# Two-step graph network on one core: attention ends without waiting for the adjacency product, ten dense blocks in layer 1, two copies per block on VectorE, and a new order

## The chip, the cores and the metric

The kernel runs on one core of a Trainium2 chip, as one launch. The metric is the device time of an execution in microseconds. The engines are called by their names in the profile: PE (TensorE, matmuls and transposes, with its weight loads as PEld), DVE (VectorE), ACT (ScalarE), POOL (GpSimd, which here issues gathers by index and adds one vector per block) and SP (SyncE, which issues the plain DMAs).

## What is computed

There are 3327 nodes with 256 features and an adjacency matrix `adj` of 3327 x 3327 that is about 0.24% full, with a full diagonal of random weights. Cut to what matters:

```python
# layer 0, h = relu(layernorm(x))
Xf = Xa = h
for n in range(2):                       # step 0 and step 1
    A  = top_p_attention(Xa)             # softmax of q k^T, entries kept to 90% of each row's mass
    Xf = R @ Xf                          # R = rows of (adj + I), normalized
    Xa = A @ Xa
    Z  = Z + Xf @ U1[n].T + Xa @ U2[n].T
x = x + layernorm(h + Z) * gamma + beta
# layer 1
h = relu(layernorm(x))
x = x + relu((D^-1/2 adj D^-1/2 @ h) @ W.T + b)
```

All arrays are float32.

## The kernel before

**Blocks.** The nodes are cut into 26 blocks of 128 rows. Each step treats the 26 blocks one after another, and each block has two halves that hardly depend on each other: the attention half and the adjacency half.

**The attention half** (kinds `ATT_0` and `ATT_1`, function `attention`). PE makes a block's logits in two groups (`lg0`, `lg1`), ACT takes their exponential (`ex0`, `ex1`; tile `e`, 128 x 3327), and the threshold that keeps 90% of each row's mass is searched: ACT passes over the whole row (`ev1r`, `ev1s`, in step 1 also `ev2s`; tile `ja`), small steps between them (`mass`, `tail`, `st1`, `sec`), then a DVE pass that cuts out a window (`win`), the largest entries of 16 pieces (`wm0` to `wm3`), a sort (`sort`), the exact cut (`cut`), and a DVE pass that drops what is not kept (`drop`). Then the 26 square pieces of the row block are transposed by PE in seven groups (`tr0` to `tr6`, tile `p_t`, two PSUM buffers), each group is copied out of PSUM (`atc0` to `atc6`, tile `at`, three buffers, all on ACT), and PE sums the products with the nodes (`att0` to `att6`, tile `att_acc`). The passes of neighbouring blocks overlap: while one block is transposed, the next one's window is cut and the one after that is evaluated.

**The adjacency half.** Since a row of `adj` has few entries, a block's columns are listed: DVE finds which of the 26 square pieces of each row are not zero and builds lists of indices (kind `LISTING`; pieces `flag`, `listA`, `owners`, `rows`), POOL gathers eight tiles of adjacency rows by index (`ga0` to `ga7`), and SP stores them to HBM (`store`, `ac_hbm`). The product loads the tiles again (`lda`), POOL gathers the eight matching tiles of node rows (`gv0` to `gv7`), and PE sums eight products (`adj0` to `adj7`, tile `adj_acc`). Sixteen tiles hold gathered node rows. In step 0 this is the kind `FIRST` (it stores `y`, which step 1 gathers, by `stxf`), in step 1 the kind `SECOND`.

**The end of a block in step 1.** `SECOND` loads `y` and the nodes `h` (`load_second`), scales its product and adds a kept product (`scale`, tile `hz_r`, one buffer), adds `h` (`resid0`) and stores the sum to `hz_hbm` (`sthz`). The attention half of the same block loads that sum (`ldh`), adds its own result (`resid0` of `ATT_1`), and goes on with the layer norm, the addition of `x`, the second norm and the nodes `hn` of layer 1 (`resid1`, `resid2`, `root1`, `xbet`, `input20` to `input23`, `root2`, `node2`, `stn`).

**Layer 1.** Eight of the blocks (`DENSE`) are computed as whole rows (kind `WHOLE`): SP loads the block's 1664 KB of adjacency (`row`), and PE sums 26 products in two parts (`first`, `second`) with the `hn` that lie in SBUF. The other 18 (kind `LATE`) use the lists: eight gathers of `hn` rows on POOL (`gath`) and eight products (`prod`). Both then transpose, multiply by W, add and store (`turn`, `mt`, `out`, `add`, `st`).

**The order.** Nothing is scheduled by the hardware or by the framework: every piece of work has a key, and the pieces are emitted in the order of their keys, which fixes the order of instructions on each engine and on SP's and POOL's queues. An engine that reaches an instruction whose input is missing waits, with all that is behind it. The key of a piece of block i is

```python
        at = BASES[kind] + PERIODS[kind] * (i if n is None else n) + (SHIFTS[kind][i] if kind < len(SHIFTS) else 0.0)
        for name, piece in do.items():
            plan.add(at + places[name], piece)
```

`PLACES` holds a place for each piece of a kind, `MOVED` other places for single blocks, and `EVENTS` single pieces (`nodes`: loading the nodes of step 1; `hn`: taking tiles for layer 1's nodes). The keys are only used for sorting. Before, `SHIFTS` has lists for the first five kinds.

Lines of the profile that are used below: L927 the ACT passes, L1126 the copies `atc`, L1120 the transposes, L1135 the attention products, L702 the sparse products, L678 and L692 the gathers of adjacency and node rows, L1106 `drop`, L1056 `wm`, L976 the first of the `tail` operations, L749 a DVE copy out of PSUM in the start of the kernel.

Of the kernel before, what the change touches and what calls it, by code (L numbers as in the profile page):

```python
# [10 lines left out]
F32 = mybir.dt.float32  # L11
# [3 lines left out]
ALU = mybir.AluOpType  # L15
AX = mybir.AxisListType

P = 128
# [30 lines left out]


# [55 lines left out]
BASES = (-1.892, 870.475, -13.053, -5.69, 853.823, -80.36, 1720.169, 1724.788)  # L106
PERIODS = (30.0573, 29.8334, 30.2195, 29.6001, 29.4593, 1.6, 11.4611, 29.3857)
ATT_0, ATT_1, LISTING, FIRST, SECOND, START, LATE, WHOLE = range(8)

DENSE = (0, 4, 7, 10, 13, 16, 19, 22)  # L110
# [8 lines left out]
        ldq=-44.287, lg0=-38.973, ex0=-25.597, lg1=-20.538, ex1=-16.452, guess0=-16.41, guess1=-16.131,  # L119
        guess2=-15.977, guess3=-15.603, guess4=-14.457, guess5=-14.33, guess6=-12.806, guess7=-12.277, ev1r=-11.76,  # L120
        ev1s=-8.469, st10=-7.961, guess8=-7.057, st11=-6.906, st12=-5.943, st13=-4.39, st14=-3.503, st15=-3.334,
        st16=-1.613, st17=0.027, thr=0.214, st18=0.892, win=3.72, cut0=7.309, wm1=9.04, wm0=10.134, wm3=10.495,
        wm2=12.344, sort0=14.201, sort1=14.201, sort2=15.126, sort3=16.348, sort4=16.684, sort5=17.022, sort6=18.245,
        sort7=18.909, sort8=19.469, sort9=19.668, cut1=19.862, cut2=20.795, cut3=21.407, cut4=22.022, cut5=22.834,
        drop=23.642, tr0=26.604, atc0=29.007, tr2=31.084, att0=32.223, atc2=32.504, tr1=33.541, atc1=35.266,
        inv=37.184, tr3=38.707, att1=40.1, tr4=41.126, atc3=41.825, att2=42.068, tr5=43.428, atc4=44.771,
        atc5=46.924, att3=47.519, tr6=48.685, atc6=50.691, att4=50.866, att5=51.309, edge=51.319, att6=52.006,
        attend=54.3, xtk_t=56.039, xtk_c=58.125, k_m=61.105, cut6=61.775, k_c=62.744, q_c=63.484, xu_m=65.976,
        xu_c=67.312, stxt=75.943, stq=77.565, stxu=81.473,
    ),  # L130
    dict(
        ldq=-120.275, lg0=-63.07, lg1=-47.295, ex0=-46.566, ex1=-41.634, guess0=-41.061, guess1=-39.487,
        guess2=-38.859, guess3=-38.65, guess4=-38.64, guess5=-37.462, guess6=-37.063, ev1s=-36.233, half=-35.672,
        mass0=-35.413, ev1r=-35.055, mass1=-32.043, tail0=-31.473, tail1=-31.053, tail2=-30.763, tail3=-28.525,
        mass2=-28.221, st10=-26.599, st11=-25.175, st12=-24.135, aux2=-23.815, ev2s=-21.461, st13=-18.043,
        btw1=-17.852, st14=-15.208, aux0=-14.988, aux1=-14.22, sec10=-12.922, sec11=-12.131, sec12=-10.743,
        thr=-7.89, sec13=-7.788, nt2=-2.992, win=2.783, wm2=6.046, wm0=6.444, wm1=6.454, wm3=6.526, sort0=8.121,
        sort1=8.162, sort2=9.437, sort3=10.527, sort4=11.217, sort5=12.023, sort6=12.773, sort7=13.564, sort8=15.249,
        cut0=15.328, sort9=15.348, cut1=16.458, cut2=17.341, cut3=18.102, cut4=18.886, cut5=19.961, cut6=20.011,
        drop=23.999, tr0=28.827, atc0=29.172, tr4=29.605, tr1=32.779, att0=32.801, tr2=32.803, atc1=33.007,  # L140
        att1=33.809, atc4=34.739, tr3=34.759, atc2=36.727, att2=37.933, tr5=38.539, tr6=39.45, atc3=40.18,
        att3=40.29, ldx=44.319, atc5=45.361, atc6=45.991, ldh=48.128, att4=48.571, inv=49.727, att5=50.339,
        att6=51.666, resid0=55.38, resid1=57.694, resid2=60.354, root1=64.136, xbet=66.296, input20=67.759,
        input21=69.483, edge=70.892, input22=73.309, input23=75.045, root2=79.569, node2=90.831, stn=94.821,
    ),
    dict(
        lda1=-109.475, flag1=-107.627, lda0=-103.644, flag0=-103.479, lda2=-99.182, flag2=-95.097, lda3=-93.033,
        flag3=-91.637, listA0=-89.556, listA1=-88.513, listA2=-87.593, listA3=-85.627, listA4=-84.042,
        listA5=-82.074, listN=-79.419, listA6=-78.234, listA7=-76.609, listA8=-73.622, before=-72.858,
        beforec=-71.255, owners0=-68.498, owners1=-67.041, owners2=-61.176, shared=-58.045, lentc=-56.671,  # L150
        rows0=-54.48, rows1=-53.784, rows2=-53.518, rows3=-52.901, rows4=-51.266, rows5=-50.983, rows6=-48.224,
        rows7=-41.568, ga1=-9.65, ga3=-5.744, ga5=-1.138, ga6=-0.012, ga7=0.9, ga4=0.953, ga2=3.801, ga0=3.89,
        store=12.996,
    ),
    dict(
        gv3=36.873, gv6=37.71, gv1=38.549, gv0=39.478, gv5=41.654, gv2=42.696, lda=49.308, ldg=49.654, gv4=49.849,
        gv7=50.182, adj0=50.797, adj1=50.94, adj2=53.03, adj3=56.206, adj4=57.968, adj5=59.203, adj6=62.128,
        adj7=63.299, roots=65.636, prop=66.557, mixy=74.549, stxf=84.692,
    ),
# [38 lines left out]
    ),  # L198
)

MOVED = {
    (0, 25): dict(
        stxt=114.064, stxu=154.091,
    ),
# [1570 lines left out]
```

## Time and profile before

| | |
|---|---|
| median of 11 runs | 1632.02 us (1624.22 to 1634.39) |
| the profiled execution | 1632.13 us, span 1630.4 us |
| mean granted clock of PE | 0.969 |
| busy: PE, DVE, ACT, POOL | 1482.1, 1219.2, 1135.4, 1035.3 us |
| chain by engine | PE 40%, ACT 32%, DVE 9%, DMA 7%, issue 4%, POOL 3% |
| moved by DMA | 272.26 MB, mean 167 GB/s |

By time, the first some 110 us prepare keys and nodes, step 0 runs to about 780, step 1 to about 1410, and layer 1 to the end. A window is a stretch of the span in us; beside it stand its length, the busy time of each engine with the number of instructions in it, the granted clock of PE, the busy share of the DMA engines and the GB/s. A row of waits names who waited, for whom, and the total, the number and the longest. A row of groups gives line, engine, operation and tiles, the count, the busy time, the mean of one in ns, and the idle time ahead of it.

### The profile page before, as it was taken

To read this page: it belongs to the slowest core of one execution; us is meant where nothing else is said; L and a number is where in the kernel's file an instruction comes from. 1 tells how busy PE (TensorE), PEld (TensorE's weight loads), DVE (VectorE), ACT (ScalarE), POOL (GpSimd) and SP (SyncE) were. 2 spreads that over 40 slices of the span, in tenths; PEclk is the share of its full clock that TensorE was granted. 3 is DMA by queue.
4 is the path that set the end of the run, shared out by engine and by line. 5 is a ranking of instruction groups with operands and counts; after the bars stand their busy time and mean duration, and the time that the engine had idled before them with its cause. 6 is when DMAs were issued, how large, how long until landed. Compare 5 with 4: busy or idle time off the path is not lost.

```text
span 1630.4 us, 24877 instructions
## 1 busy us (share of the span) xinstructions
PE 1482.1 (91%) x7372; PEld 1158.3 (71%) x7372; DVE 1219.2 (75%) x3963; ACT 1135.4 (70%) x2692; POOL 1035.3 (64%) x808
## 2 busy tenths in 40 slices
PE   4967999979999998998589999999999999999996
PEld 2535787767778777786367777777777777888784
DVE  4579999779999997984389888988898889601111
ACT  2657777757787786873789999999999998200000
POOL 0058888788888888887455665466556564067774
PEclk9968999989999999999889999999999999999998
DMA  6556867666566765544433334343343344377763
GB/s 183 172 166 196 271 208 230 197 192 211 165 196 197 221 209 176 165 133 160 158 119 124 122 96 126 119 125 95 112 136 117 109 138 138 127 238 267 256 190 117
DMA packets 149167, 272.26 MB, mean 167 GB/s; under 512 B 29603, under 2 KB 94496, under 8 KB 148000
## 3 DMA queue, kind: packets, MB, share of 16 engines
q1 hardware_dynamic: 109456, 181.58, 34.1%
q0 software_dynamic: 33536, 87.08, 18.5%
q10 hardware_dynamic: 6032, 1.93, 0.5%
q8 instruction: 60, 0.98, 0.2%
q14 instruction: 83, 0.68, 0.1%
HBM read 221.08 MB, written 49.41 MB: 166 GB/s over the span
## 4 chain that ended last, share of the span: by engine, by line
PE 40%; ACT 32%; DVE 9%; DMA 7%; issue 4%; POOL 3%; DVEq 0%; SPq 0%; POOLq 0%; ACTq 0%
PE att_acc L1135 14%; ACT ja L927 13%; ACT e L883 5%; PE late_sums L1544 5%; PE adj_acc L702 4%; PE p_t L1120 4%; PE p_l L866 4%; ACT at L1126 4%; PE late_acc L702 3%; DMA ac<-in_adj_t,a_idx 3%; POOL ac L678 2%; DVE cand L1056 2%; DMA vg<-hn_hbm,v_idx 2%; DMA vg<-gb_hbm,v_idx 1%; DVE e L1106 1%
## 5 line engine op out<-in xcount | busy, mean ns | idle before, releaser
L692 POOL DMA_INDIRECT vg<-y_hbm,v_idx x208 | 321.0, 1543 | 245.4 <-PE adj_acc L702 181.1
L927 ACT ACTIVATE ja<-e,t 128x3327 uint8<-128x3327 f32 x127 | 389.6, 3068 | 0.7
L678 POOL DMA_INDIRECT ac<-in_adj_t,a_idx x208 | 282.1, 1356 | 147.5 <-DVE own L619 84.4
L1135 PE MATMUL att_acc<-h,at 128*128 128x256 f32 (+1 forms) x1352 | 324.2, 386 | 0.0
L1135 PE MATMUL att_acc<-xa,at 128*128 128x256 f32 (+1 forms) x1352 | 320.7, 381 | 0.2 <-DVE hz L1250 0.2
L692 POOL DMA_INDIRECT vg<-gb_hbm,v_idx x208 | 268.2, 1289 | 63.4 <-issue 39.6
L1135 PEld LDWEIGHTS att_acc<-h,at 128*128 128x128 f32 (+1 forms) x1352 | 252.8, 193 | 41.0 <-issue 7.6
L1135 PEld LDWEIGHTS att_acc<-xa,at 128*128 128x128 f32 (+1 forms) x1352 | 251.8, 191 | 31.6 <-DVE hz L1250 0.4
L1126 ACT COPY at<-p_t 128x512 f32<-128x512 f32 (+1 forms) x364 | 196.8, 545 | 94.6 <-PE p_t L1120 89.2
L1120 PE MATMUL p_t<-ident,e 128*128 128x128 f32 x1352 | 208.4, 280 | 36.0 <-ACT at L1126 21.3
L1056 DVE MAX8 cand<-w 128x8 f32<-128x208 f32 x832 | 238.5, 358 | 0.2
L702 PE MATMUL adj_acc<-vg,ac 128*128 128x257 f32 (+1 forms) x832 | 230.1, 389 | 8.8 <-DMA vg<-gb_hbm,v_idx 6.2
L1120 PEld LDWEIGHTS p_t<-ident,e 128*128 128x128 f32 x1352 | 162.4, 143 | 93.3 <-ACT at L1126 33.0
L866 PE MATMUL p_l<-kt,q 64*128 64x512 f32 (+1 forms) x832 | 183.9, 558 | 30.0 <-ACT e L883 27.8
L1049 DVE SCALAR_TENSOR_TENSOR w<-e,t 128x3327 f32<-128x3327 f32 x52 | 191.1, 3676 | 19.9 <-ACT t L897 19.6
L1106 DVE SCALAR_TENSOR_TENSOR e<-e,kept 128x3327 f32<-128x3327 f32 x52 | 191.9, 3691 | 0.5
L883 ACT ACTIVATE e<-p_l 128x2048 f32<-128x2048 f32 x104 | 161.6, 1554 | 18.8 <-PE p_l L866 16.8
L702 PEld LDWEIGHTS adj_acc<-vg,ac 128*128 128x128 f32 x832 | 148.4, 192 | 34.6 <-issue 8.6
L692 POOL DMA_INDIRECT vg<-hn_hbm,v_idx x144 | 136.8, 950 | 54.6 <-issue 33.9
L866 PEld LDWEIGHTS p_l<-kt,q 64*128 64x128 f32 x832 | 75.5, 193 | 113.2 <-issue 67.6
L730 ACT COPY xt_k<-p_turn 128x256 f32<-128x256 f32 x52 | 19.0, 369 | 155.8 <-PE p_turn L726 154.3
L570 DVE TENSOR_REDUCE most<-adj_sb 128x7 f32<-128x896 f32 x104 | 105.2, 1012 | 4.8 <-DMA adj_sb<-in_adj_t 4.0
(443 smaller groups left out, 1924.5 us busy)
## 6 DMA issues: line engine op xcount, KB each, us to landing
ac<-ac_hbm SPq DMA_DIRECT2D x70, 512.0 KB
adj_sb<-in_adj_t SPq DMA_DIRECT2D x78, 448.0 KB
ac_hbm<-ac SPq DMA_DIRECT2D x26, 512.0 KB
adj_row<-in_adj_t SPq DMA_DIRECT2D x8, 1664.0 KB
adj_sb<-in_adj_t SPq DMA_DIRECT2D x26, 320.0 KB
gb_hbm<-gb SPq DMA_DIRECT2D x26, 256.0 KB
gb<-gb_hbm SPq DMA_DIRECT2D x26, 256.0 KB
q<-q_hbm SPq DMA_DIRECT2D x104, 32.0 KB
```

Of the source, the lines that this page charges most:

```text
L678: nc.gpsimd.indirect_dma_start(s["list"][:, k, :], None, adj_rows, bass.IndirectOffsetOnAxis(ap=s["a_idx"][:, k : k + 1], axis=0))
L692: nc.gpsimd.indirect_dma_start(t[:, :D], None, hbm[:, :], bass.IndirectOffsetOnAxis(ap=v_idx[:, i, k : k + 1], axis=0))
L702: nc.tensor.matmul(s["acc"][:, :width], s["ac"][:, k, :], rows[:, :width], start=(k == 0), stop=(k == SLOTS - 1))
L866: nc.tensor.matmul(pl[:, at : at + cw], s["q"][rows, :], kt[rows, c0 + c : c0 + c + cw], start=True, stop=True)
L883: nc.scalar.activation(halves(s["e"])[:, :, c0 : c0 + w], logits_of(s.pop(("l", g)))[:, :, :w], AF.Exp, accum_out=s["zp"][:, g : g + 1],)
L927: nc.scalar.activation(junk, s["e"][:, :N], f, bias=s["t"], scale=-1.0, accum_out=s[name])
L1049: nc.vector.scalar_tensor_tensor(w[:, :N], ev, s["t"], ev, op0=ALU.is_le, op1=ALU.mult, accum_out=s["below"])
L1056: nc.vector.max(s["cand"][:, 8 * n : 8 * n + 8], s["w"][:, c0 : c0 + cw])
L1106: nc.vector.scalar_tensor_tensor(ev, ev, kept8[:, step * NB + i, 0:1], ev, op0=ALU.is_ge, op1=ALU.mult, accum_out=den)
L1120: nc.tensor.transpose(pt[:, c : c + P], s["e"][:, b * P : (b + 1) * P], ident)
L1126: nc.scalar.copy(at[:, :w], pt[:, :w])
L1135: nc.tensor.matmul(s["att"][:, :D], at[:kb, c : c + P], v[b][:kb, :D], start=(b == 0), stop=(b == NB - 1))
```

## The change

- In step 1 the copies `atc2` and `atc5` of each block are made by DVE (`AT_VECTOR`).
- For blocks 0 to 19 (`FLIPS = 20`) the end of the block is turned around: the attention half no longer loads the product's sum but `h`, adds its result and stores that to `hz_hbm`; a new kind `NORM`, with keys of its own, loads it, adds it to the product's sum (now in two buffers), and does the norms and the rest. For blocks 20 to 25 the end stays with the attention.
- `DENSE` has ten blocks, 12 and 24 are added; 16 blocks stay with the lists.
- Every base, period, place, shift and event is new. The shifts of `FIRST` now rise from 10 to 173 and those of `SECOND` fall from 159 to 8 (53 for the last block), where both changed little over the blocks; those of `LISTING` rise from 55 to 106, where they fell from 49 to 19. `NORM` falls from 154 to -97 over its 20 blocks. `START`, `LATE` and `WHOLE` have shifts too.

```diff
+AT_VECTOR = (2, 5)
-BASES = (-1.892, 870.475, -13.053, -5.69, 853.823, -80.36, 1720.169, 1724.788)
-PERIODS = (30.0573, 29.8334, 30.2195, 29.6001, 29.4593, 1.6, 11.4611, 29.3857)
-ATT_0, ATT_1, LISTING, FIRST, SECOND, START, LATE, WHOLE = range(8)
-DENSE = (0, 4, 7, 10, 13, 16, 19, 22)
+BASES = (-1.211, 869.963, -13.315, 19.408, 853.008, -80.36, 1725.639, 1718.681, 871.362)
+PERIODS = (30.045, 29.955, 30.2736, 28.584, 29.0064, 1.6, 11.2176, 30.9758, 29.9036)
+ATT_0, ATT_1, LISTING, FIRST, SECOND, START, LATE, WHOLE, NORM = range(9)
+FLIPS = 20
+DENSE = (0, 4, 7, 10, 13, 16, 19, 22, 12, 24)
...
-        gv3=36.873, gv6=37.71, gv1=38.549, gv0=39.478, gv5=41.654, gv2=42.696, lda=49.308, ldg=49.654, gv4=49.849,
-        gv7=50.182, adj0=50.797, adj1=50.94, adj2=53.03, adj3=56.206, adj4=57.968, adj5=59.203, adj6=62.128,
+        gv7=-7.92, gv1=0.845, gv0=10.048, gv5=14.251, gv6=26.524, gv3=43.864, gv4=44.513, gv2=46.75, lda=47.649,
+        adj0=53.814, adj1=55.177, adj2=55.686, ldg=57.795, adj3=58.657, adj4=59.088, adj5=60.784, adj6=62.621,
...
-    keys=-32.591, centre=764.748, roots=817.644, hn=827.229, nodes=878.278, last_nodes=918.935, hn_last=1606.3,
+    keys=-23.287, centre=778.673, nodes=824.15, last_nodes=913.762, hn=1041.506, roots=1047.764, hn_last=1290.252,
...
-    def attend_copy(s, g):
+    def attend_copy(s, g, step):
         pt = s.pop(("pt", g))
         s["at"][g] = at = work.tile([P, 512], F32, name="at", bufs=3)
         w = (min(4 * g + 4, NB) - 4 * g) * P
-        nc.scalar.copy(at[:, :w], pt[:, :w])
+        if step == 1 and g in AT_VECTOR:
+            nc.vector.tensor_copy(at[:, :w], pt[:, :w])
+        else:
+            nc.scalar.copy(at[:, :w], pt[:, :w])
...
-        for name, hbm, tag in (("y", y_hbm, "xf1"), ("h", h_hbm, "hl")):
+        for name, hbm, tag in (("y", y_hbm, "xf1"), ("h", h_hbm, "hl"))[: 1 if i < FLIPS else 2]:
...
-        r["hz"] = work.tile([P, D], F32, name="hz_r", bufs=1)
+        r["hz"] = work.tile([P, D], F32, name="hz_r", bufs=2)
...
+    def load_attended(i, r):
+        r["h"] = work.tile([P, D], F32, tag="hl", name="h", bufs=2)
+        nc.sync.dma_start(r["h"], hz_hbm[i * P : (i + 1) * P])
+
+    def attended_node(i, t):
+        hz = t["hz"]
+        nc.vector.scalar_tensor_tensor(hz, t.pop("att")[:, :D], t["inv"], hz, op0=ALU.mult, op1=ALU.add)
+        yield
+        nc.sync.dma_start(hz_hbm[i * P : (i + 1) * P], t.pop("hz"))
...
-        nc.sync.dma_start(t["hz"], hz_hbm[i * P : (i + 1) * P])
+        nc.sync.dma_start(t["hz"], (h_hbm if i < FLIPS else hz_hbm)[i * P : (i + 1) * P])
...
-        do["resid0"] = lambda: add_node(r)
-        do["sthz"] = lambda: store_residual(i, r)
+        if i >= FLIPS:
+            do["resid0"] = lambda: add_node(r)
+            do["sthz"] = lambda: store_residual(i, r)
+        return do
+
+    def normalized(i, s, hn):
+        do = {}
+        do["ldz"] = lambda: load_attended(i, s)
+        do["plus"] = lambda: add_node(s)
+        do["ldx"] = lambda: s.update(x=load_x(i))
+        do["xbet"] = lambda: add_bet(s)
+        in_steps(do, "resid", 2, lambda: moments_in_steps(s, s["hz"]))
+        do["root1"] = do["root2"] = lambda: root_moments(s["n"])
+        in_steps(do, "input2", 4, lambda: input_2(i, s))
+        do["node2"] = lambda: node_2(i, s, hn[i])
+        do["stn"] = lambda: store_2(i, s, hn[i])
         return do
...
+        do["ldh"] = lambda: load_residual(i, s)
+        if i < FLIPS:
+            in_steps(do, "resid", 2, lambda: attended_node(i, s))
+            return do
...
             plan_block(plan, SECOND, i, products_1(i, state[SECOND, i]))
             plan_block(plan, ATT_1, i, block_1(i, state[ATT_1, i], xa1, kt2, hn))
+            if i < FLIPS:
+                plan_block(plan, NORM, i, normalized(i, state[SECOND, i], hn))
```

## The prediction

> **What bounds the kernel now.** I read the page's busy shares and its forty slices first, to see where no engine is full; then the table of windows by stage; then the chain and the waits of each stage; then the costliest groups, for prices. The profiled execution took 1632.13 us around a span of 1630.4, and the median of the runs shown is 1632.02, so a change of the span is read straight as a change of the median. About 0.2% (3.3 us) is what a measurement of this kernel can tell from no change.
>
> ```profile
> PE 1482.1 (91%) x7372; PEld 1158.3 (71%) x7372; DVE 1219.2 (75%) x3963; ACT 1135.4 (70%) x2692; POOL 1035.3 (64%) x808
> PE   4967999979999998998589999999999999999996
> DVE  4579999779999997984389888988898889601111
> ACT  2657777757787786873789999999999998200000
> POOL 0058888788888888887455665466556564067774
> ```
>
> There are three regimes: step 0 (slices 3 to 18), where PE and DVE are both high, step 1 (slices 20 to 33), where ACT stands at 9, and layer 1 (from slice 34), where only PE and POOL work.
>
> ```profile
> core 0: us, PE busy (x) PEld busy (x) DVE busy (x) ACT busy (x) POOL busy (x), PEclk, DMA share, GB/s
> 125.50:758.50 633.00, 594.47 (x3094) 469.57 (x3094) 563.12 (x1846) 469.41 (x1169) 514.77 (x389) 0.98 0.62 195
> 221.50:605.50 384.00, 364.26 (x1907) 288.96 (x1904) 349.41 (x1150) 289.91 (x723) 311.79 (x238) 0.99 0.64 200
> 888.50:1282.50 394.00, 378.63 (x1938) 296.48 (x1937) 348.90 (x1140) 382.40 (x850) 228.77 (x153) 1.00 0.39 118
> 1371.90:1421.40 49.50, 48.02 (x249) 41.37 (x248) 36.55 (x123) 17.88 (x45) 2.18 (x3) 1.00 0.38 125
> ...
> 1431.50:1611.50 180.00, 170.99 (x798) 144.48 (x796) 29.35 (x65) 11.61 (x33) 136.27 (x144) 1.00 0.71 230
> 1611.50:1630.40 18.90, 6.67 (x19) 4.68 (x18) 2.33 (x6) 0.37 (x1) 0.49 (x1) 0.61 0.14 45
> ```
>
> The first window runs from the first to the last pass of step 0 that drops the unkept entries; the second holds 15 of its blocks (25.6 us each, DVE busy 23.3: the time is 1.10 of the fullest engine). The third holds 17 blocks of step 1: 23.18 us each, ACT busy 22.49, DVE 20.52; the time is 1.03 of the fullest engine. In 1431.5 to 1611.5 POOL issues 144 gathers in 180 us, 1.25 us each without a gap, and after the last of them 18.9 us follow in which PE has 19 matmuls: layer 1 ends by POOL.
>
> ```profile
> by line: PE att_acc L1135 24.1%; PE adj_acc L702 8.0%; DMA ac<-in_adj_t,a_idx 7.6%; issue 6.6%; PE p_t L1120 6.6%; PE p_l L866 6.5%; DVE cand L1056 4.3%; DVE e L1106 3.5%; DMA vg<-gb_hbm,v_idx 2.9%; POOL vg L692 2.7%; POOL ac L678 2.6%; ACT
> ```
>
> This is the chain in the first window. Gathers are on it (7.6 + 2.9% as transfers, 2.7 + 2.6% as issues): 15.8% of 633, some 100 us. That is why step 0 runs at 1.10 and not at 1.03.
>
> ```profile
> DVE tail_d L976 <- ACT mass L897: 34.4, 17, 3.0
> L1126 ACT COPY at<-p_t 128x512 f32<-128x512 f32 x102 | 57.7, 566 | 0.3 <-PE p_t L1120 0.3
> L749 DVE COPY xt_key<-p_turn 128x256 f32<-128x256 f32 x26 | 10.8, 415 | 0.6 <-PE p_turn L726 0.2
> ```
>
> In the step 1 window DVE waits 2.0 us per block for ACT, once per block, and ACT waits for nobody: ACT sets step 1.
>
> **Step 0: the lag of the first half (term A).** The key of FIRST's block i grows by 28.584 plus its shift, 35.1 per block over the step, where the attention's grows by 29.4; before, 29.4 against 29.8. Counted in the order that the keys give, 160 of the first half's products stand ahead of step 0's last drop, where 196 did: 36 x 2 matmuls of 0.216 us (26 took 5.61) are 15.6 us off PE, 10 DVE operations of 0.48 are 5 us off DVE, and 33 node and 18 adjacency gathers are 51 x 1.25 = 64 us off POOL. DVE stays the fullest at 558. What matters is the distance: adjacency tiles are gathered, stored and loaded again, and the product that reads them stood under one block behind its attention; now it stands two behind at block 5 and five at block 20, and the node gathers' keys spread over 55 units, where they spread over 13. The gathers' 100 us on the chain can give back nothing (633 stays as 1.124 of DVE's work: -5) or all down to step 1's ratio (558 x 1.03 = 575: -58). I take a quarter, -25: SP's stores and loads of these tiles still stand in one queue, and with PE at 94% the chain falls to PE at once. The moved halves go to the passage between the steps, where three slices of PE (733 to 856 us) show 8, 5 and 8; ACT is full there, so they cost nothing as long as they don't stand ahead of its logits on PE.
>
> **Step 1: copies, second half, block ends (term B).** Two of seven copies leave ACT: 2 x 0.566 = 1.13, so 22.49 becomes 21.4 (21.5 with what is left of the first halves). No DVE copy of 128x512 is in the trace; by 128x256 (0.415) and 64x128 (0.288, the other copy from PSUM) 128 columns are 0.127, so 512 are 0.67; the bounds are 0.415 and, twice the smaller, 0.83. DVE becomes 20.52 + 1.34. The second half now starts about five blocks late and runs at 1.18 per attention block (160 products in 17 blocks for 136), for DVE +0.17: 22.0. PE: 52 matmuls of attention at 0.216 (11.2), 26 transposes at 0.11 (four in 0.60, two in 0.38: 2.9), 16 + 4 of the half (4.3), logits 3.0 (eight in 1.92, eight in 1.35, the ends overlapping): 21.4, and 0.18 x 4.3 more: 22.2 at most. So ACT 21.5, DVE 22.0, PE 22.2, for ACT 22.5 alone. At 1.03 of DVE's 22.0 a block takes 22.7, at 1.10 (engines that wait for each other, as in step 0) 24.2; I take 22.7, since in step 1 nothing waits for a gather: 0.48 x 25 = -12, bounds -24 (22.2, PE without a gap) and +26.
>
> [...]
>
> PE's busy row says 378.63/17 = 22.27. [...] By the busy row PE would be the fullest at 23.0, times 1.03 is 23.7, and B would be +13; by the counted matmuls it is -12.
>
> The 20 split block ends hold the same operations: the product's sum, one addition, the same moments and scaling. Stores and loads are as many (h is loaded by the attention, the sum stored and loaded once, as before). Cost nothing; what covers them is ACT's and DVE's other blocks. New is that the attention waits for no product. Behind the load of the stored sum on SP stand other blocks' queries; if that store is late they wait, up to the 15.7 us that SP waits at worst for that store now. The sum's second buffer is what lets the product run one block ahead; it and the later point at which hn takes its tiles cost nothing.
>
> **Layer 1 (term C).** Two blocks more are dense: 2 x 8 gathers and 2 x 16 matmuls go, 2 x 52 matmuls and 2 row loads come. POOL: 128 x 1.25 = 160 us, -20. PE: 104 - 32 = 72 x 0.216 = +15.6. Counted, PE had 8 x 52 + 18 x 16 + 26 x 4 matmuls and 52 turns, 180 us, from 1421.4 on: free by 1602, then it waited for the last gathers and ended its last product at 1616. Now it has 195.8; 5.6 of that (13 blocks of one dense sum) stand before the last block's attention, where 1.5 us were idle. 1421.4 + 195.8 - 1.5 = 1616, with POOL done at 1592. From the last product to the span's end are 14.5 us, before as after. So C = 0: the 20 us that POOL gives go to PE, which becomes the bound. Bounds: -6 (PE's start of the dense sums moves up by the 5.6) and +9 (PE keeps the 9 us of holes that it has in 1431.5 to 1611.5).
>
> **Sum.** 1632.1 - 25 - 12 + 0 = 1595.
>
> **Rivals.** (1) *Gathers stay on the chain, and three full engines eat the copies' gain*: A -5, B 0 (a ratio of 1.05), C 0: 1627. For it: DVE's work in step 0 falls by under 1%. Against: POOL loses 64 us of 515 ahead of the last drop. Chance 0.17. (2) *The gathers vanish from the chain*: A -50, B -20, C 0: 1562. Chance 0.12. (3) *Slower: a DVE copy that waits for its transposes holds the engine.* One copy stands ahead of the next block's window (3.7 us), the other ahead of the next drop; behind it wait the tail operations on which ACT's next pass depends. In step 0 ACT's copies wait 58.8 us for p_t in 56 cases, 1.05 each and 3.6 at most. With w per copy a block takes 22.7 + 2w; it decides from 2w = 1.5 (37 us in 25 blocks, what A and B give together). With w = 1.3 a block takes 25.3: +53 - 25 = 1660. Against: in DVE's order some 2 us of small work lie between the drop and the first copy, as long as two transposes and a copy take. Chance 0.14. (4) Parts cancel within 3 us: 0.04. My forecast has 0.53.
>
> **Numbers.** Faster are the forecast, (2) and half of (1): 0.53 + 0.12 + 0.09 = 0.74; same is the rest of (1) and (4): 0.12; slower 0.14. For 8 in 10 I reach down to 1560, about the middle of (2), and up to 1642, which leaves most of (3) out.
>
> **What would show it.** Right: DVE, ACT and PE all over 93% in step 1 with a block at 22.7; the share of gathers on step 0's chain under 12%, and the last drop of step 0 at 733; POOL's last gather over 30 us before the end, with PE full up to the last dense product. Wrong: DVE waiting for p_t over 1 us a copy; a step 1 block over 23.2; the last drop of step 0 no earlier than 755; PE idle over 15 us between its first dense sum and its last product.

## The result, and the profile after

The changed kernel takes 1688.84 us (median of 8 runs, 1683.74 to 1692.47) where the kernel before takes 1630.55 (31 runs): a ratio of 1.0354, 95% interval 1.034 to 1.0369. It is slower by 58 us; forecast were 37 us less.

The page of the profile after, shares of the engines and the forty slices:

```profile
PE 1507.9 (89%) x7444; PEld 1172.9 (69%) x7444; DVE 1258.8 (75%) x4013; ACT 1119.1 (66%) x2642; POOL 958.6 (57%) x792
...
PE   4775898998898899988679899999999999999996
...
DVE  4349889887989898976388889989999999711212
ACT  2456686776678777872688999888989998200000
```

The shares say little: PE, DVE and ACT have about the work that they had, POOL less. The windows show the stages (lengths in us, then busy time per engine):

```profile
core 0: us, PE busy (x) PEld busy (x) DVE busy (x) ACT busy (x) POOL busy (x), PEclk, DMA share, GB/s
143.00:779.00 636.00, 579.44 (x3003) 456.35 (x3004) 565.48 (x1817) 462.69 (x1139) 454.80 (x354) 0.98 0.59 183
811.00:1011.00 200.00, 166.08 (x786) 121.58 (x786) 152.80 (x459) 174.67 (x381) 89.60 (x70) 0.91 0.32 99
1033.00:1407.00 374.00, 358.28 (x1814) 280.35 (x1813) 342.68 (x1090) 336.75 (x756) 242.62 (x184) 1.00 0.49 147
1488.00:1660.00 172.00, 169.35 (x800) 146.71 (x799) 25.32 (x62) 10.12 (x29) 121.66 (x128) 1.00 0.70 235
```

The first is step 0 from its first to its last drop, as before. The second is the beginning of step 1, in which almost no second half runs (the first sums its products from 978 us on, the next from 1002), and the third is 15 blocks of step 1 with them, 24.93 us each. The fourth is layer 1, PE full.

The drop passes of DVE are good milestones. By their starts the 58.8 us between the two spans divide as in the first two rows of this table, which has every kernel that was run but one (the time is a median; the stages are in us of the profiled execution: step 0 and step 1 each from its first to its last drop, the passage between them, the rest behind the last drop; a block is the mean distance of the first exponentials of blocks 10 to 25 in step 1):

| kernel | time, ratio to before (95%) | to first drop | step 0 | passage | step 1 | rest | block |
|---|---|---|---|---|---|---|---|
| before | 1630.55 | 125.3 | 632.9 | 67.6 | 576.3 | 228.3 | 23.22 |
| after | 1688.84, 1.0354 | 142.8 | 636.4 | 76.6 | 605.3 | 228.1 | 24.94 |
| new_order_old_start | 1672.71, 1.0249 (1.0206 to 1.0291) | 123.8 | 636.4 | 76.8 | 605.3 | 228.4 | 24.98 |
| new_order_act_copies | 1696.34, 1.0399 (1.0379 to 1.0419) | 139.9 | 636.2 | 76.8 | 611.3 | 229.2 | 25.14 |
| new_order_eight_dense | 1688.41, 1.0354 (1.0327 to 1.0382) | 141.7 | 635.3 | 76.8 | 604.9 | 225.1 | 24.93 |
| new_order_earlier_halves | 1726.76, 1.0571 (1.0549 to 1.0592) | 139.9 | 633.8 | 81.9 | 640.8 | 228.5 | 26.54 |
| new_order_half_products | 1683.3, 1.0315 (1.0295 to 1.0334) | 139.3 | 635.7 | 76.8 | 602.4 | 228.4 | 24.90 |
| new_order_light_ends | 1686.98, 1.0342 (1.0321 to 1.0363) | 138.9 | 634.7 | 76.8 | 604.3 | 228.4 | 24.92 |
| new_order_half_copies | 1677.5, 1.0279 (1.0257 to 1.0301) | 142.0 | 636.0 | 76.8 | 593.8 | 227.9 | 24.54 |
| new_order_all_light | 1669.13, 1.0226 (1.0205 to 1.0247) | 142.7 | 635.3 | 76.8 | 586.3 | 227.6 | 24.33 |
| old_order_copies | 1738.81, 1.0649 (1.0604 to 1.0694) | 123.8 | 635.0 | 68.1 | 683.3 | 226.8 | 28.00 |
| old_order_copies_ahead | 1711.15, 1.0481 (1.0457 to 1.0505) | 125.1 | 632.2 | 67.7 | 657.8 | 228.8 | 26.17 |
| old_order_one_copy | 1629.07, 0.9988 (0.9978 to 0.9999) | 125.4 | 630.6 | 65.1 | 575.0 | 227.4 | 23.18 |
| old_order_third_copy | 1948.31, 1.053 (1.0482 to 1.0579) | 126.0 | 808.1 | 63.4 | 679.5 | 270.3 | 27.77 |
| old_order_split_ends | 1671.04, 1.0238 (1.0213 to 1.0262) | 123.6 | 634.0 | 68.3 | 614.2 | 229.0 | 25.06 |
| old_order_ends_in_place | 1917.9, 1.0371 (1.0326 to 1.0417) | 126.1 | 804.6 | 62.1 | 646.9 | 275.2 | 26.42 |
| old_order_late_halves | 1693.22, 1.0368 (1.0322 to 1.0413) | 125.9 | 634.4 | 61.9 | 645.4 | 227.4 | 26.96 |
| old_order_ten_dense | 1642.86, 1.0061 (1.0041 to 1.0082) | 123.8 | 634.1 | 68.8 | 578.8 | 235.7 | 23.22 |
| old_order_all_parts | 1759.7, 1.0783 (1.0737 to 1.0828) | 124.1 | 634.1 | 68.4 | 695.2 | 235.7 | 28.28 |

So after against before: +17.5 ahead of the first drop, +3.5 in step 0, +9.0 in the passage, +29.0 in step 1, nothing behind it. The two kernels at 1948 and 1918 us ran on a chip on which the kernel before takes 1847 us. Their step 0 and their rest are longer by some 170 and 45 us, about what that chip costs the kernel before (215); their times are read as ratios, and no profile shows the kernel before on that chip.

Most of the passage's 9 us can be read in the order. In the changed kernel the first exponential of step 1 starts 31.4 us after the last drop of step 0, before 23.2. Its logits are made by 803 us, but it stands in ACT's order behind `xa`, the result of step 0's last block, which waits for PE's products; before, it stood ahead of that one.

```profile
809.25 0.47 ACT L1246 ACTIVATE xa<-att_acc,inv 128x256 f32<-128x256 f32 x1 [5.54 <-PE att_acc L1240]
810.60 1.88 ACT L985 ACTIVATE e<-p_l 128x2048 f32<-128x2048 f32 x1
```

The chain is shown for the changed kernel with eight dense blocks, whose order up to layer 1 is the same, since in the changed kernel itself it is followed back only to 1388 us. In step 0 (142 to 777 us):

```profile
by line: PE att_acc L1262 25.3%; PE p_t L1244 8.6%; PE adj_acc L826 7.8%; PE p_l L990 7.0%; issue 5.6%; ACT ja L1051 5.5%; DVE e L1230 4.6%; DVE cand L1180 4.0%; ACT at L1253 3.3%; DVE most L694 2.6%; ACT e L1007 2.6%; PE p_xu L1332 2.3%; D
```

The gathers, 15.8% of this chain before, have nearly left it: none is among the rows down to 2.3%, and all of theirs add up to 3.3%. In their place stand ACT's passes and copies above all (ACT has 16.2% of this chain, before 9.2), and PE's work, the transposes most (54.2%, before 49.6); DVE has 18.5%, before 18.1. The stage is not shorter. In step 1, before (950 to 1350 us) and in that kernel (1044 to 1378):

```profile
by line: ACT ja L927 36.2%; ACT e L883 10.7%; ACT at L1126 10.0%; PE att_acc L1135 7.1%; PE p_l L866 2.4%; ACT t L897 2.1%; PE p_t L1120 1.9%; ACT u L897 1.7%; issue 1.7%; ACT bn_rr L430 1.6%; ACT ln L429 1.5%; PE adj_acc L702 1.5%; ACT mas
```

```profile
by line: ACT ja L1051 18.6%; PE att_acc L1262 12.4%; issue 11.0%; DVE cand L1180 10.3%; PE adj_acc L826 6.5%; PE p_l L990 5.2%; ACT e L1007 2.9%; PE p_t L1244 2.6%; ACT at L1253 2.5%; DVE cand L1193 2.1%; PE adj_acc L1351 1.9%; DVE val L119
```

Before, one engine carries the chain: 36.2 + 10.7 + 10.0% in three rows of ACT. After, ACT, PE and DVE hand it round ("issue" holds most of DVE's long passes). That is what a stage looks like that no engine bounds alone.

### The profile page after: what moved, and what is told of

Its sections match the earlier page's. It is cut to its first block, busy times and chain, and to the rows that moved or that the text cites. A ratio compares the mean times of both kernels' runs of the same rounds, so it can differ in the third digit from the quotient of the medians.

```text
span 1689.2 us, 25018 instructions
## 1 busy us (share of the span) xinstructions
PE 1507.9 (89%) x7444; PEld 1172.9 (69%) x7444; DVE 1258.8 (75%) x4013; ACT 1119.1 (66%) x2642; POOL 958.6 (57%) x792
## 3 DMA queue, kind: packets, MB, share of 16 engines
q0 software_dynamic: 32768, 84.98, 17.5%
## 5 line engine op out<-in xcount | busy, mean ns | idle before, releaser
L794 POOL DMA_INDIRECT vg<-y_hbm,v_idx x208 | 277.8, 1335 | 227.3 <-PE adj_acc L804 128.5
L780 POOL DMA_INDIRECT ac<-in_adj_t,a_idx x208 | 263.1, 1265 | 131.5 <-issue 65.1
L1240 PE MATMUL att_acc<-h,at 128*128 128x256 f32 (+1 forms) x1352 | 327.8, 386 | 3.4 <-ACT at L1231 3.2
L1222 PE MATMUL p_t<-ident,e 128*128 128x128 f32 x1352 | 211.8, 283 | 73.3 <-ACT at L1231 23.4
L1231 ACT COPY at<-p_t 128x512 f32<-128x512 f32 (+1 forms) x312 | 168.1, 541 | 118.0 <-PE p_t L1222 102.2
L804 PE MATMUL adj_acc<-vg,ac 128*128 128x257 f32 (+1 forms) x832 | 226.5, 387 | 3.3 <-DMA ac<-ac_hbm 3.3
L985 ACT ACTIVATE e<-p_l 128x2048 f32<-128x2048 f32 x104 | 161.4, 1552 | 35.1 <-PE p_l L968 23.9
L794 POOL DMA_INDIRECT vg<-hn_hbm,v_idx x128 | 121.7, 951 | 62.0 <-PE late_acc L804 22.9
```

Of the source, the lines that this page charges most:

```text
L780: nc.gpsimd.indirect_dma_start(s["list"][:, k, :], None, adj_rows, bass.IndirectOffsetOnAxis(ap=s["a_idx"][:, k : k + 1], axis=0))
L794: nc.gpsimd.indirect_dma_start(t[:, :D], None, hbm[:, :], bass.IndirectOffsetOnAxis(ap=v_idx[:, i, k : k + 1], axis=0))
L804: nc.tensor.matmul(s["acc"][:, :width], s["ac"][:, k, :], rows[:, :width], start=(k == 0), stop=(k == SLOTS - 1))
L985: nc.scalar.activation(halves(s["e"])[:, :, c0 : c0 + w], logits_of(s.pop(("l", g)))[:, :, :w], AF.Exp, accum_out=s["zp"][:, g : g + 1],)
L1222: nc.tensor.transpose(pt[:, c : c + P], s["e"][:, b * P : (b + 1) * P], ident)
L1231: nc.scalar.copy(at[:, :w], pt[:, :w])
```

## The experiments

"Old order" means the changed code with the tables (places, shifts, moved pieces, events) of the kernel before; "new order" is the changed kernel. Five theories met: (1) the second halves come some 160 us late (the first one's sum is scaled at 992 us, where it was at 833) and then run at 1.36 per attention block, which overfills PE; (2) the copies on DVE cost, by place (2a) or by themselves (2b); (3) the split block ends cost; (4) a block is a loop through DVE and ACT; (5) three engines over 90% full hold one another.

**The start.** *new_order_old_start:* the places and shifts of `START` and its event as before.

```diff
+PLACES[START], SHIFTS[START], EVENTS["keys"] = those of before
```

> The changed kernel with the places and shifts of the kernel's start (making queries, keys and values of step 0) and its one event as before. If the 17.5 us that the first drop comes later are the start's order alone and nothing later absorbs them, 1671 us with 4 either way and a first drop near 126 us; if the stretched order of step 0's first block makes them, or step 0 is bound elsewhere, 1689 with 4 either way.

It came: 16.1 us back, the first drop at 123.8. Windows of the start, after and then before:

```profile
40.00:60.00 20.00, 17.83 (x71) 9.93 (x70) 11.36 (x33) 10.80 (x30) 0.00 (x0) 1.00 0.44 147
60.00:80.00 20.00, 14.50 (x54) 7.62 (x53) 4.31 (x17) 8.43 (x22) 0.00 (x0) 0.96 0.34 109
```

```profile
40.00:60.00 20.00, 19.36 (x82) 11.33 (x81) 13.43 (x42) 12.15 (x38) 0.00 (x0) 1.00 0.59 181
60.00:80.00 20.00, 19.40 (x82) 11.33 (x81) 7.93 (x28) 13.20 (x36) 0.00 (x0) 1.00 0.54 166
```

Before, PE was full in the start: 164 instructions in these 40 us, against 125 after. Now it waits there for copies that stand later in ACT's order (the weight loads of `start_sums` for `kt`: 13.9 us between 20 and 100 us). Nothing behind absorbs it.

**The copies.** *old_order_copies:* only the two copies on DVE. *old_order_copies_ahead:* the same, the next block's window and maxima behind the first copy. *old_order_one_copy, old_order_third_copy:* one copy each.

```diff
-AT_VECTOR = ()              # before
+AT_VECTOR = (2, 5)          # old_order_copies, and old_order_copies_ahead, which has
+        win=7.4, wm2=7.5, wm0=7.6, wm1=7.7, wm3=7.8,   # for 2.783, 6.046, 6.444, 6.454, 6.526
+AT_VECTOR = (5,)            # old_order_one_copy
+AT_VECTOR = (2,)            # old_order_third_copy
```

> The order and the parts of the kernel before, with only the two copies per block of step 1 on VectorE. Theory 1 (PE is the limit in step 1, at 96% of the time busy where ACT is 97%) expects little: ACT falls by 1.1 us per block and DVE rises by 1.36, but PE stays at 22.3 us of busy time per block: 1632 with -12 to +5. Theory 2 expects DVE at 21.9 plus its waits for ACT (2.0 us per block) to set a block at 23.9: +18, 1650.

> The kernel before with only the two copies per block of step 1 on VectorE, as in the run of that name without 'ahead', but the next block's window pass and its first maxima stand behind the first of these copies in DVE's order (window 2.78 to 7.4, maxima 6.0 to 6.5 to 7.5 to 7.8). Theory 2a (the loss of 107 us is the place: a copy queued behind a window pass of 3.7 us, with PE and then ACT waiting for it) expects most of it back: 1660 or less. Theory 2b (the copy on DVE costs by itself) expects 1720 or more.

> The kernel before with only the sixth copy of each block of step 1 on VectorE (the third stays on ScalarE). In DVE's order the sixth stands among the small operations of the next block's sort, not behind its window pass. If the place behind the long pass made the loss of 107 us, this gains what ACT loses, up to 0.57 x 25 = 14 us, or is the same: 1618 to 1635. If any copy put into DVE's order makes PE wait, 1650 or more.

> The kernel before with only the third copy of each block of step 1 on VectorE, the one that stands behind the next block's window pass and its maxima in DVE's order. If the place makes the loss, this loses what both copies lost: 1730 with 10 either way. If the two copies lose together only, 1650 or less.

Two copies alone cost 107 us, far beyond both theories' numbers. The waits of old_order_copies from 1000 to 1400 us, and a piece of its chain (start, length, what):

```profile
ACT e L1048 <- PE p_t L1285: 65.5, 15, 7.0
...
PE att_acc L1303 <- DVE at L1292: 41.3, 13, 4.9
```

```profile
1028.59 3.52 issue
1032.22 1.21 DVE cand L1221 x4
1033.43 0.60 DVE at L1292
1034.07 1.99 PE att_acc L1303 x8
```

The copy stands behind the window pass (its 3.5 us show as "issue") and the maxima in DVE's order. PE waits for it, once per block and up to 4.9 us, and the next logits stand behind PE's wait, so ACT waits 4.4 us per block (65.5 in 15) where it had waited for nobody. The third copy alone does nearly all of it (27.77 us per block against 28.00, and 1.053 of its chip's kernel before against 1.0649), the sixth, among short operations, nothing: 2a, and one_copy is the only kernel here that beats both, though by no more than 2 us (its interval ends at 0.9999). Moving the window behind the copy gives back 28 of the 107 us, where 2a expected 72 or more: DVE now waits for transposes (25.8 us in 10 waits from 1000 to 1400) and ACT for the moments behind it. So the place is the cause, but pushing one piece back does not mend it.

*new_order_act_copies:*

```diff
-AT_VECTOR = (2, 5)
+AT_VECTOR = ()
```

> The changed kernel with all copies of step 1 back on ScalarE, nothing else. Theory 1 (PE is filled in step 1 by 1.36 halves per attention block) expects 1689 with 8 either way: DVE gives 1.36 us per block, which it doesn't need, and ACT goes from 22.4 to 23.5 us per block of 24.9. Theory 2 (the copies on DVE are what makes step 1 slower, as they do in the old order) expects a step 1 block near 23.5 and 1655 or less.

Slower by 7.5 us. In the new order the copies gain. From 1044 to 1393 us of the changed kernel DVE hardly waits for their transposes, and they take what was priced (0.67 us):

```profile
L1229 DVE COPY at<-p_t 128x512 f32<-128x512 f32 x28 | 19.0, 680 | 1.7 <-PE p_t L1222 1.7
```

**The split ends and the late halves, in the old order.** *old_order_split_ends:* 20 split ends, with the changed kernel's places for `NORM` and a shift of 8; by the keys that is more than 8 behind the old places: the addition and the moments stand 18 to 20 units later (`plus` at 65.0 + 8 + 0.9, where `resid0` stood at 55.4). *old_order_ends_in_place:* the pieces from `root1` on where they were, but the addition and the moments at 64.0 to 64.1, where they had 55.4 to 60.4. *old_order_late_halves:* split ends, with the second halves and ends as late as in the changed kernel.

```diff
+FLIPS = 20; hz_r with bufs=3           # all three; AT_VECTOR = () and eight dense blocks
+SHIFTS[NORM] = 8.0                     # old_order_split_ends
+BASES, PERIODS, SHIFTS[NORM] = those of ATT_1; ldz=57.9, plus=64.0, resid0=64.05, resid1=64.1, from root1 on as before   # ends_in_place
+tables of SECOND and NORM, events hn and roots = those of after                             # late_halves
```

> The order and the parts of the kernel before, with only the 20 split block ends (the end follows the second half, its places 8 us after the old ones, three buffers of the sum). Theory 3 (the split ends cost by themselves, through the sum's way over HBM and SP's queue) expects 1645 or more. Theories 1 and 2 expect 1632 with 6 either way, since the operations are the same and ACT sets step 1.

> The kernel before with only the 20 split block ends, as in the run old_order_split_ends (1671 us), but each piece of the end at the place it had before, some 10 to 15 us earlier; the addition of the product's sum stands 6 us behind the store that its load waits for. If the later place made the 39 us, most come back: 1645 or less. If the way over HBM makes them, DVE now waits for that load, and the time is 1665 or more.

> The order of the kernel before in the start, step 0, the attention of step 1 and layer 1; all copies on ScalarE, eight dense blocks; 20 block ends go with the second half, and the second halves and these ends have the late places of the changed kernel. Theory 1 expects the loss of step 1 to appear with no copy on VectorE: some 24.9 us per attention block from block 10 on instead of 23.2, 25 to 38 us in all, 1657 to 1670 us. Theory 2 expects 1632 with 8 either way, since DVE has no copies.

The split ends at these places cost 39 us with the same operations, 24.54 us per block for blocks 3 to 10 and 25.06 from block 10 on. At the earlier places they cost more (1.0371 against 1.0238 of each chip's own kernel before); there the wait turned up on ACT (1100 to 1500 us), and DVE's order shows what it waits for:

```profile
ACT ln L598 <- DVE bn_mv L614: 42.5, 15, 4.2
```

```profile
1207.85 3.67 DVE L1218 SCALAR_TENSOR_TENSOR w<-e,t 128x3327 f32<-128x3327 f32 x1
...
1211.45 0.42 DVE L1411 TENSOR_TENSOR hz_r<-hz_r,h 128x256 f32<-128x256 f32 x1
1211.90 0.43 DVE L611 BATCH_NORM_STATS2 bn_st<-hz_r 128x6 f32<-128x256 f32 x1
1212.37 0.18 DVE L614 BATCH_NORM_AGGREGATE bn_mv<-bn_st 128x2 f32<-128x6 f32 x1
```

ACT loses 2.8 us per block to moments that stand behind the window pass: at 64.0 the addition comes just after the window of the block two further on, where at 55.4 it stood ahead of it, and in 14 of the 15 blocks it follows that pass on DVE without a gap. That is the copies' fault once more, the place. DVE waits for no load in these stretches of either run, though old_order_ends_in_place expected it if the way over HBM cost; so that reason of theory 3 is not shown. No run has the moments of a split end ahead of the window pass, so what the split costs apart from its place stays open. At the later place ACT's largest wait is for transposes (14.5 us in 17 cases from 1000 to 1400; before the change 0.3 in one, from 950 to 1350); what makes those late is not settled.

Late halves and ends cost 22 us on top of these, with no copy on DVE: 24.00 us per block for blocks 3 to 10, 26.96 from block 10 on, when the halves run. That they cost, theory 1 has right; the time came out over its 1657 to 1670, since the split's cost was not in it, and the late places were not tried without the split.

**Ten dense blocks.** *old_order_ten_dense* and *new_order_eight_dense:*

```diff
+DENSE = (0, 4, 7, 10, 13, 16, 19, 22, 12, 24), tables of LATE and WHOLE of after   # old_order_ten_dense
+DENSE = (0, 4, 7, 10, 13, 16, 19, 22), tables of LATE and WHOLE of before          # new_order_eight_dense
```

> The kernel before with only ten dense blocks in layer 1 (with the new places of layer 1). The forecast's term C expects 0, with -6 and +9 as bounds: 1632, 1626 to 1641. If layer 1 gains the 20 us that POOL gives, 1612.

> The changed kernel with eight dense blocks and the old places of layer 1. Term C of the forecast says 0 for ten dense blocks: 1689 with 5 either way. By the run in the old order, where they cost 11 us, 1678.

No gain in either order: +10.8 in the old, of which 2.5 in step 1 and 7.4 behind it by the table, and 0 within the error in the new (1688.41 against 1688.84; behind the last drop the ten take 228.1 us and the eight 225.1).

**All parts in the old order.** *old_order_all_parts:* copies, split ends and ten dense blocks.

```diff
+tables of START, LISTING, FIRST, SECOND, ATT_0, ATT_1 and the events of before; SHIFTS[NORM] = 8.0
```

> The changed code with all its parts (20 block ends with the second half, two copies on VectorE in step 1, ten dense blocks) but with the places, shifts and periods that the kernel before had for the start, both steps and the events; layer 1 keeps the new places, the sum has a third buffer. Theory 1 (the order costs: the second halves start some 160 us late, PE is left unfilled around the passage and overfilled afterwards, 1.36 halves per attention block) expects at most 1632 us, since the halves run beside every attention block again, and step 1 (last drop of step 0 to last drop of step 1) at 644 us or a few less, against 682. Theory 2 (the copies make DVE too full) expects step 1 no shorter than 670 us and at least 1655. Theory 3 (the split block ends cost by themselves) expects the same as theory 2, with waits of DVE and SP for stored sums.

A plain miss: 1760, not 1632 or less. The parts themselves cost 128 us in the old order (107, 39 and 11 singly), and the new order gives 71 of them back, though its start costs 16. So it isn't the new order that makes these parts dear; it makes bearable what costs more in the old one.

**Earlier halves in the new order.** *new_order_earlier_halves:*

```diff
 SHIFTS[FIRST][i]  -= 70 * i / 25
 SHIFTS[SECOND][i] -= 70 * (1 - i / 25)     # NORM too, no earlier than the store that it loads
 EVENTS["hn"], EVENTS["roots"] = 1000, 1001 # for 1041.5 and 1047.8
```

> The changed kernel with the first half of step 0 growing late by 93 units instead of 163 over the step, and the second half starting 70 units earlier and lagging less in proportion (the ends with it). The y of the last block should be there some 60 us earlier, and the second halves run at about 1.17 per attention block instead of 1.36. Theory 1, in the form that the crowding of halves and ends makes a step 1 block long, whatever engine it fills, expects a block at 23.9 in place of 24.9 and 1672 with 8 either way. If the crowding doesn't matter, 1689 with 5 either way.

The last `y` came at 875 us, not 928, and the first second half at 938, as meant; but a block took 26.5 us, and the time rose by 38, against both numbers expected. The crowding was less (18 halves in the 14 blocks that held 19) and the blocks longer, so the number of halves per block is not what a block's length follows alone. That pieces put between others that weren't moved cost more than the spreading gave is a guess; no run shows it.

**What fills a block of step 1 in the new order.** Four kernels that leave work out, and one that does three of these at once.

```diff
+    if k < 4: matmul(...)                                        # half_products, in SECOND
+    c0, cw = WIN_COLS[n][0], WIN_COLS[n][1] // 2                 # half_maxima, in step 1
+    if i >= FLIPS: scalar_tensor_tensor(...)   # twice           # light_ends, in input_2
+    w = (min(4 * g + 4, NB) - 4 * g) * P // 2                    # half_copies, in step 1
     # all_light: the first, third and fourth edit
```

> The changed kernel with only four of the eight products of each second half of step 1 (the other four are left out of the sum; their gathers, loads and all else stay). That takes 104 matmuls of 0.216 us off PE, 22.5 us, most of them in the stretch where PE is 96% busy. Theory 1 (PE sets that stretch) expects 15 to 22 us less, 1667 to 1674, and DVE over 95% busy in its place. Theory 2 (DVE sets it) expects 1689 with 4 either way.

> The changed kernel with the maxima of the window in step 1 taken over half of each piece's columns (the other half of the columns is left out). By 128x208 such a maximum took 0.358 us; by 104 columns it should take some 0.25, so 16 x 0.11 = 1.7 us per block come off DVE, 45 us in 26 blocks. Theory 1 (PE sets step 1) expects 1689 with 6 either way. Theory 2 (DVE sets it, by its load) expects 1.7 x 16 blocks = 27 us less, 1662 or below.

> The changed kernel with two DVE operations of 0.5 us left out of each of the 20 split ends (the second norm's scaling and the addition of x; layer 1 gets other numbers, the work is the same). That is 1.3 us per attention block off DVE in the crowded stretch, 20 us in all. Taking 1.2 us per block off PE had left the block at 24.9. Theory 4 (a block's length there is a loop through DVE and ACT, into whose queues the ends are put) expects 12 to 20 us less, 1669 to 1677. Theory 5 (three engines over 90% full hold one another, none alone decides) expects 1689 with 5 either way.

> The changed kernel with the copies of step 1 cut to half their width on both engines (the products read the copied half twice; the attention's output is another, the work of PE the same). By 128x256 against 128x512 the row of the copy on DVE goes from 0.68 to 0.42, on ACT from 0.57 to about 0.36: ACT loses 1.0 us per block, DVE 0.5. Theory 5 (three engines over 90% full hold one another) expects little, PE being left at 96%: 1684 with 6 either way. If ACT alone sets the block, 1.0 x 16 = 16 us less, 1673.

> The changed kernel with all three reliefs: four of eight products of each second half of step 1, two DVE operations less in each split end, and copies of half the width in step 1 (what each leaves out is told with its own run). PE loses 1.2 us per block of the crowded stretch, DVE 1.8, ACT 1.0. Theory 5 expects a block some 1.0 to 1.5 us shorter where each relief alone gave nothing: 23.4 to 23.9 for 24.9, and 15 to 25 us in all, 1664 to 1674. If the order or a transfer sets the block, 1684 with 5 either way, the sum of what they gave singly (5 and 2).

half_maxima took 9655 us, because with half the columns the kernel's own test at the end finds a row whose window hid an entry, and computes the network again in another way. Its first computation can still be read: the maxima came down from 358 to 251 ns,

```profile
L1161 DVE MAX8 cand<-w 128x8 f32<-128x104 f32 x210 | 38.2, 251 | 0.2
```

and step 1 from its first to its last drop took 601 us (852 to 1453), where it takes 605.3. So 1.7 us per block off DVE gave 4 us in all; half_products gave 3 (its other 3.5 us lie ahead of the first drop), and light_ends, with 1.0 us per block less on DVE, gave 1. The windows of half_products and of all_light, 15 blocks each:

```profile
1028.00:1401.00 373.00, 330.76 (x1649) 252.09 (x1647) 343.49 (x1090) 335.95 (x755) 247.93 (x184) 0.99 0.49 147
```

```profile
1024.00:1389.00 365.00, 330.91 (x1651) 253.97 (x1651) 321.53 (x1055) 322.78 (x757) 250.27 (x184) 0.99 0.50 151
```

In the first PE has come down from 358 to 331 us for 15 blocks, 1.8 us each, DVE and ACT stand where they stood (343 and 336 us), and the block went from 24.94 to 24.90. Where PE's time went can be read in its waits, in the third window of the changed kernel and in that of half_products:

```profile
PE p_t L1222 <- ACT at L1231: 8.0, 16, 1.6
```

```profile
PE p_t L1226 <- ACT at L1235: 25.9, 29, 2.6
```

Freed of products, PE waits longer for ACT's copies, which free the two buffers that the transposes write. Theory 1 as "PE sets it" and theory 2 as "DVE's load sets it" fall, and so does theory 4, which expected 12 to 20 us of light_ends (it gave 1.9). half_copies, which takes work off ACT and DVE, gave 11.5 us of step 1 (1677.5, just below theory 5's 1684 with 6 either way, and 4.5 above what ACT alone would give), and all three reliefs 19.0, against 15.4 for the three singly (2.9, 1.0, 11.5). By the medians the sum is nearer still: 19.7 together, 18.7 singly. So theory 5 has the time of all_light right (1669), but neither its reason, that single reliefs give little and all together much more, nor the block: 24.33, where 23.4 to 23.9 were expected. The copies are the load that counts most; what ACT's share in it is and what DVE's, this run doesn't tell. With everything lightened the fullest engine is busy 331 of 365 us, and the rest of the 24.3 us is waiting. The largest of PE's waits there is again the one for ACT's copies (22.1 us in 18 cases); what makes up the rest stays open.

## Why the prediction was wrong, point by point

**Step 0 (A: -25).** The mechanism happened: POOL fell from 515 to 455 us, and the gathers fell to 3.3% of the chain, far under the 12% that was to show it. The gain did not: +3.5. The step that failed is the weighing of what the gathers' 100 us on the chain can give back, nothing or all down to step 1's ratio: "I take a quarter". The end "nothing" (633 stays) was the right one. The time of the gathers on the chain was not time to be gained: other work, ACT's and PE's above all, was nearly as late and took their place. DVE's work, put at 558, was 565.48, and the stage is 1.125 of it, the ratio of before. The last drop fell at 779, not 733; past 755 the forecast had called itself wrong.

**What was not costed.** The new order of the start, +17.5 (16.1 by its own run): the change was listed in front of the forecast, and it got no term. The passage was to cost nothing "as long as they don't stand ahead of its logits on PE": it took 9.0 more, most of it since its first exponential stands on ACT behind the result of step 0's last block.

**Step 1 (B: -12).** The copy was priced right (0.67, measured 0.680). Rival 3's sign, DVE waiting for `p_t`, is absent (1.7 us in 28 copies). Two steps failed. "Runs at 1.18 per attention block" is a mean over a stretch that isn't even: almost no half up to block 7, then 19 halves and 18 ends in 14 blocks, 1.36. And "1.03 of DVE's 22.0": the third window has DVE at 342.68/15 = 22.85, and 24.93 is 1.09 of that, close to the ratio of step 0, which the forecast had kept as its bad bound (+26; measured +29). The reason given for 1.03, that nothing waits for a gather, does not bear on it: PE, DVE and ACT, each busy 90 to 96% there, wait for each other in many short waits (PE for ACT's copies 8.0 us in 16 waits, DVE for ACT's `rd` 8.2 in 7, ACT for DVE's `shift` 6.3 in 11, none over 2.4). That they do so because they are full is not shown, for with load taken off all three the time rose from 1.04 to 1.10 of the fullest one's (374/358 and 365/331); what sets the block stays open. The assumption that the 20 split ends cost nothing failed as well: in the old order, at the places tried, they cost 39.

**The two weighings of PE.** PE's busy row would have made B +13, nearer than -12, but by luck: with PE's busy time down to 331 of 373 us a block was as long (24.90 us for 24.94). The counted matmuls (22.2 us a block at most), taken in place of the row, were the author's estimate; in the third window PE is busy 358.28/15 = 23.89 us a block.

**Layer 1 (C: 0).** Right: 228.1 for 228.3 us from the last drop to the end, POOL's last gather 29 us before the end (over 30 was the sign), PE busy 169.35 of 172 us up to it.

**The rivals.** The slower one had a mechanism close to what the copies do in the old order, but turned round: not DVE waits for the transposes, PE waits for a copy behind DVE's long pass, and ACT for PE. Its price (w = 1.3, +53) was half of the 107 us there. In the changed kernel that loss was ordered away. Its 58 us are the start (17.5), step 0 (3.5), the passage (9.0) and step 1 (29.0). For the 29 the split and late ends are the likeliest source, since they cost 39 and 22 in the old order; but no run takes them out of the new one, so that is argued and not shown.

## What to carry to other kernels

In this kernel, whose order is fixed by hand, an operation's price was its place more than its length: two copies of 0.68 us, one of them behind a pass of 3.7 us, cost 4.8 us per block, and the other one alone, among short operations, nothing. Moments put behind the same pass made ACT wait 2.8 us per block. With the gathers down from 15.8 to 3.3% of step 0's chain the stage took 635.3 us (new_order_eight_dense) for 632.9: before counting on a releaser's removal, look for the work that would end last without it. And give every reordered stage a term, the start too.

## What the runs showed of the hardware

PE's granted clock was lower where PE waited more. Step 1 before, and with the two copies in the old order (21 blocks each, nearly the same number of matmuls):

```profile
842.00:1329.00 487.00, 469.00 (x2400) 367.36 (x2399) 428.01 (x1400) 471.95 (x1047) 282.17 (x189) 1.00 0.39 119
```

```profile
842.00:1426.00 584.00, 507.58 (x2407) 393.04 (x2406) 455.89 (x1473) 455.90 (x1004) 272.40 (x189) 0.93 0.33 101
```

At a clock of 1.00 a matmul took 469.00/2400 = 0.195 us of busy time, at 0.93 0.211: 8% more, 38.6 us of busy time in these 21 blocks. In these 584 us the trace's clock records show 0.5 fifteen times, for 3.4 or 6.8 us each and 78.5 us in all (half of that is 39 us, about the busy time gained), each time around the end of a gap of 3.0 to 4.9 us in PE's work, and 1.0 otherwise. Before, they show 1.0 in all of the 487 us, in which no gap in PE's matmuls is over 1.6 us. So PE's own work was longer where it waited; no run takes the wait and the clock apart. In the changed kernel the stretch almost without second halves (811 to 1011 us) shows 0.91, with records of 0.5 for 34.1 us, the crowded one (1033 to 1407) 1.00, with none.
